# Flamingo block: the last quarter of the attention output added by VectorE from the PSUM bank, one operand sum moved ahead of a multiplication, and another finish of the last group

## The chip, the core and the metric

The kernel runs on one core of a Trainium2 chip. A core has a matrix engine (TensorE, PE in the profile, with its weight loads PEld), three elementwise engines (VectorE or DVE, ScalarE or ACT, GpSimd or POOL) and SyncE (SP), whose queue issues transfers. Each engine works through its own queue in order and waits on semaphores for the others. The metric is the time on the device, in microseconds; the median of three runs of the kernel before is 1302.78 us (1302.33 to 1303.58).

## What is computed

The reference, cut to what matters:

```python
def xattn(x, context, Wq, Wk, Wv, Wo, bo):           # 16 heads of 64
    q, k, v = heads(x @ Wq), heads(context @ Wk), heads(context @ Wv)
    attn = softmax(q @ k.T / 8)
    return merge(attn @ v) @ Wo + bo
def ffn(x, W, b, logits, u):
    idx = argmax(log_softmax(logits) - log(-log(u)))
    return x @ W[idx] + b[idx]
y   = x + tanh(g_xattn) * xattn(layernorm(x), ctx_768)
out = y + tanh(g_ffn)   * ffn(layernorm(y))
```

x has 4 x 2048 rows of 512 features, the context 4 x 77 rows of 384, all in float32.

## The kernel before

**Groups.** The 8192 rows of x are worked through in 16 groups of 512 rows. Rows tiles (`xg`, `ys`, `ts_`) hold rows on partitions, column tiles (`xc`, `pT`) hold features on partitions; VectorE's 32x32 block transposes lead from one to the other (`to_columns`, `to_rows`). The head projections are folded into matrices ahead of the groups: `m` (x to the scores of all heads) and `vo` (probabilities to the attention output), so that a group is three matmuls: scores (`ps_s`), attend (`ps_a`) and the feed-forward part (`ps_f`).

**Seven products.** Each of the three is done by a scheme with seven block products in place of eight (class `Seven`). The moving operand is cut into four blocks: B11, B12, B21, B22, the first digit half of the contraction, the second half of the group's 512 rows. GpSimd forms four sums of them (`Columns.sum`, line 437):

```python
a, b_, op = dict(T1=("B12", "B11", ALU.subtract), T2=("B22", "T1", ALU.subtract),
                 T3=("B22", "B12", ALU.subtract), T4=("B21", "T2", ALU.subtract))[name]
```

The products go in the order B11, T1, T2, B21, T3, B22, T4 (`ORDER`) into three PSUM banks. The four quarters of the result (11, 22, 12, 21: output half, then row half) become ready one after another. `post(s)` evicts after product s: after products 0, 1, 2 and 6 ScalarE copies a bank into the tile `snap` (`keep`; for attend with the bias `bo_c`, as two activations, line 473; otherwise line 469); after 3, 4 and 5 VectorE adds a bank to what is in `snap` (line 486). Quarter 21 is the last; it is the whole bank `ps[0]` after product 6.

**A group.** The main loop (i = 1 to 15, j = i-1, f = i-2) runs the scores of group i, the attend of group j, whose softmax was done before, and the feed-forward of group j. While the attend products run, ScalarE forms the exponentials of group i head by head (`exps`, line 532), VectorE sums each of four head sets (`head_sum`, lines 539 and 540), and GpSimd multiplies by the reciprocals (`head_scale`, line 543). VectorE then transposes the probabilities into columns for the next attend (`p_columns`, line 552). When quarters of the attend are ready, GpSimd adds them to the columns of x, which turns `xc[j]` into y (`residual`, line 558), then forms T1 to T4 of y for the feed-forward, while `y_rows` transposes y to rows for the second layernorm and the last addition. The seventh feed-forward product runs in the next group (`end_of_ff`).

The order of all this is written out by hand: the statements after `at.product(s)` and `ff.product(s)` fix the place of each instruction in its engine's queue. What follows the attend of a group is lines 868 to 881: on VectorE the sum of the last heads; on GpSimd residual 12, T1, T2, residual 21, the last heads' multiplication, T3, T4. Groups 3, 7 and 11 also reload `m` and form its block sums (`weight_sum`, line 124), one of them on VectorE at line 869.

**The end.** After the loop, lines 907 to 947 do the attend of the last group, lines 949 to 970 its feed-forward, with the layernorm statistics of y between the products: `mean` and `var` each put a small matmul (`ps_st`, line 375) into PE's queue; `rstd` ends in a power on GpSimd (line 409). Lines 972 to 981 then scale the feed-forward rows, add them to y and store: rows blocks 8 to 15 by ScalarE and GpSimd, 0 to 7 by VectorE in eight fused operations (line 976), in twelve DMAs on the queues of SyncE and ScalarE.

Of the kernel before, what the change touches and what calls it, by code (L numbers as in the profile page):

```python
# [10 lines left out]
AF = mybir.ActivationFunctionType  # L11
ALU = mybir.AluOpType
AX = mybir.AxisListType

P = 128
# [4 lines left out]
def flamingo_block_kernel(  # L20
# [43 lines left out]
    NA = 4  # L64
# [55 lines left out]
    def weight_sum(w, n, engine=None):  # L120

        to, a, b_, op = ((5, 0, 3, ALU.subtract), (3, 3, 2, ALU.add), (4, 3, 0, ALU.subtract),
                         (6, 1, 4, ALU.subtract))[n]
        (engine or nc.gpsimd).tensor_tensor(flat(w[:, to]), flat(w[:, a]), flat(w[:, b_]), op)  # L124
# [430 lines left out]
    def residual(j, at, which, engine=None):  # L555

        c = xc[j].at["B" + which]
        (engine or nc.gpsimd).tensor_tensor(c, c, at.quarter(which), ALU.add)  # L558

    def y_rows(j, q0, v=None):  # L560
        if j not in ys:
            ys[j] = row_tile("y")
        for q in (q0, q0 + 1):
            c = xc[j].all[:, q, :]
            to_rows(ys[j], c if v is None else c[:, ts(v, T2)], q, v)
# [190 lines left out]
    for i in range(1, NGRP):  # L756
        j, f, nx = i - 1, i - 2, i + 1
        n = norms[i]
        last = nx == NGRP
        swap_m, swap_vo = i % GPB == GPB - 1 and not last, 1 < i and j % GPB == 0  # L760
        if 1 < i:

            s0 = scores0(i)
            for s in range(6):
                s0.product(s)
                if s == 0:
                    s0.post(0)
                    if 0 <= f:
                        end_of_ff(f)
                    p_columns(j, 6, 8)  # L770
                    xc[i].sum("T4")
                if s == 1:
                    p_columns(j, 8, 10)
                    if 0 <= f:
                        f_rows(f, ff, 1)
                if s == 2:
                    pT[j].sum("T1")
                    pT[j].sum("T3")
                if 0 < s:
                    s0.post(s)  # L780
                if 0 <= f and s in (2, 3):
                    n.stats(ys[f], 0, 8 * (s - 2), 8)
                if s == 3 and 0 <= f:
                    add_bias(f, nc.gpsimd)
            for k in range(2):
                s_rows(i, k, s0.chunk(0, k))

            s1 = Seven("ps_s", w_scores, xc[i], (2, 3), SNAP)
            s2 = Seven("ps_s", w_scores, xc[i], (4,), SNAP1)
            for s in range(7):  # L790
                s1.product(s)
                s2.product(s)
                if s == 0:
                    s1.post(0)
                    s2.post(0)
                    s0.product(6)
                    s0.post(6)
                    n.mean()
                    for k in range(2):
                        s_rows(i, KH + k, s0.chunk(1, k))  # L800
                elif s < 4:
                    norm_step(n, s)
                if swap_vo and 3 <= s:
                    weight_sum(vo, s - 3, nc.vector if s < 5 else None)
                if 5 <= s and 0 <= f:
                    f_scale(f, n.rs, 5 * (s - 5), 5)
                if 0 < s:
                    s1.post(s)
                    s2.post(s)
                if s == 5:  # L810
                    for k in range(2):
                        s_rows(i, 2 + k, s1.chunk(0, k))
                    s_rows(i, 4, s2.chunk(0, 0))
            for k in range(2):
                s_rows(i, KH + 2 + k, s1.chunk(1, k))
            s_rows(i, KH + 4, s2.chunk(1, 0))
            if swap_m:
                load_m(nx // GPB)
        if not last:
            norms[nx] = Norms(nx)  # L820


        at = Seven("ps_a", w_attend, pT[j], (0, 1), SNAP, bo_c)
        for s in range(7):
            at.product(s)
            if s == 0:
                pT[j].sum("T2")
                if 0 <= f:
                    f_scale(f, n.rs, 10, 6)
                    f_add(f, 0, NG, nc.gpsimd)  # L830
                    store(f)
                head_max(i, 0)
                head_max(i, 1)
            if s == 1:
                head_max(i, 2)
                head_max(i, 3)
            if 1 <= s:
                e = (0, 10, 20, 32, 44, 56, 64)
                exps(i, e[s - 1], e[s])
            if s == 0 and i == 1:  # L840
                weight_sum(vo, 3)
                pT[j].sum("T3")
            if s == 1 and i == 1:
                scale_wf(wfr)
            if s == 2:
                pT[j].sum("T4")
                if swap_m:
                    weight_sum(m, 0)
                if not last:
                    x_columns(nx)  # L850
                    norms[nx].stats(xg[nx], norms[nx].x0, 0, 8)
                head_sum(i, 0)
                head_scale(i, 0)
            if s == 3:
                if not last:
                    norms[nx].stats(xg[nx], norms[nx].x0, 8, 8)
                    if nx + 1 < NGRP:
                        load(nx + 1)
            if s == 4:
                residual(j, at, "11")  # L860
                head_sum(i, 1)
                head_scale(i, 1)
            if s == 5:
                head_sum(i, 2)
                head_scale(i, 2)
                residual(j, at, "22")
            if s == 6:
                if swap_m:
                    weight_sum(m, 1, nc.vector)
                head_sum(i, 3)  # L870
                residual(j, at, "12")
            at.post(s)
        if j % GPB == GPB - 1:
            load_vo((j + 1) // GPB)
        yc[j] = Columns(xc[j].all, **{f"T{k + 1}": tq[:, k] for k in range(4)})
        yc[j].sum("T1")
        yc[j].sum("T2")
        residual(j, at, "21")
        head_scale(i, 3)
        yc[j].sum("T3")  # L880
        yc[j].sum("T4")


        ff = Seven("ps_f", w_ffn, yc[j], (0, 1), SNAP)
        for s in range(6):
            ff.product(s)
            if s < 2:
                y_rows(j, 2 * s)
            if not last:
                if s == 1:  # L890
                    xc[nx].sum("T1")
                if s == 2:
                    xc[nx].sum("T2")
                if s == 4:
                    if swap_m:
                        weight_sum(m, 2)
                    xc[nx].sum("T3")
                    if swap_m:
                        weight_sum(m, 3)
            if 2 <= s:  # L900
                k = (0, 2, 3, 5, 6)
                p_columns(i, k[s - 2], k[s - 1])
            ff.post(s)
        f_rows(j, ff, 0)
# [6 lines left out]
    for s in range(7):  # L911
# [24 lines left out]
            store(f)  # L936
        if s == 6:
            residual(j, at, "12")
            for q in (0, 2):
                y_rows(j, q, 1)  # L940
        if 0 < s:
            at.post(s)
    yc[j] = Columns(xc[j].all, **{f"T{k + 1}": tq[:, k] for k in range(4)})
    yc[j].sum("T1")
    yc[j].sum("T2")
    residual(j, at, "21")
    yc[j].sum("T3")
    yc[j].sum("T4")
    n = Norms(NGRP + 1)
    ff = Seven("ps_f", w_ffn, yc[j], (0, 1), SNAP)  # L950
    for s in range(7):
        ff.product(s)
        if s == 0:
            n.stats(ys[j], 0, 8, 8)
            y_rows(j, 0, 0)
        if s == 1:
            y_rows(j, 2, 0)
            n.stats(ys[j], 0, 0, 8)
            add_bias(j, nc.gpsimd)
        if s == 3:  # L960
            n.mean()
            n.spread()
        if s == 4:
            n.var()
            n.rstd()
        ff.post(s)
        if s == 4:
            f_rows(j, ff, 1, 1)
        if s == 5:
            f_rows(j, ff, 0, 1)  # L970
            f_rows(j, ff, 0, 0)
    f_scale(j, n.rs, 8, 8)
    f_rows(j, ff, 1, 0)
    f_add(j, 8, 8, nc.gpsimd)
    for g in range(8):
        nc.vector.scalar_tensor_tensor(ys[j][:, g, :], ts_[j][:, g, :], n.rs[:, g : g + 1], ys[j][:, g, :],
                                       ALU.mult, ALU.add)
        if g == 3:
            store(j, 0, 4, (nc.scalar, nc.sync))
    store(j, 8, 8, (nc.scalar, nc.sync))  # L980
    store(j, 4, 4, (nc.sync, nc.scalar))


# [39 lines left out]
```

## Time and profile before

| what | value |
| --- | --- |
| median of 3 runs | 1302.78 us |
| the profiled execution | 1302.34 us, span 1300.4 us |
| PE busy | 1260.2 us, 97% of the span |
| POOL, DVE, ACT busy | 894.2, 884.8, 651.6 us |
| granted TensorE clock, mean | 0.993 |
| one group, start of a product to the same one of the next | 73.57 us |
| POOL sums T1 to T4 of 128x512 (line 437) | 1.27 us each |
| POOL residual of 128x512 (line 558) | 1.33 us mean of 64 |
| POOL multiplication of one head set (line 543) | 2.27 us |
| last matmul ends, span ends | 1288.7, 1300.4 us |

Times in profile rows are microseconds from the start of the span. A row of the timeline gives the start, the time covered, the engine, the line, the operation, what it writes and reads, and how many instructions were merged into it; square brackets hold the idle time ahead of it and what ended it. Matmul ends are modelled, so a row of PE reaches a little over the start of the next. A float32 matmul of the program is two instructions; one feed-forward product is eight of them.

### The profile page before, as it was taken

To read this page: it belongs to the slowest core of one execution; us is meant where nothing else is said; L and a number is where in the kernel's file an instruction comes from. 1 tells how busy PE (TensorE), PEld (TensorE's weight loads), DVE (VectorE), ACT (ScalarE), POOL (GpSimd) and SP (SyncE) were. 2 spreads that over 40 slices of the span, in tenths; PEclk is the share of its full clock that TensorE was granted. 3 is DMA by queue.
4 is the path that set the end of the run, shared out by engine and by line. 5 is a ranking of instruction groups with operands and counts; after the bars stand their busy time and mean duration, and the time that the engine had idled before them with its cause. 6 is when DMAs were issued, how large, how long until landed. Compare 5 with 4: busy or idle time off the path is not lost.

```text
span 1300.4 us, 16961 instructions
## 1 busy us (share of the span) xinstructions
PE 1260.2 (97%) x5780; PEld 1068.9 (82%) x5780; DVE 884.8 (68%) x1823; ACT 651.6 (50%) x1766; POOL 894.2 (69%) x495
## 2 busy tenths in 40 slices
PE   9999869999999999999999999999999999999996
PEld 5666658888888888888888888888888888888885
DVE  6669776766667676766667676666767676666556
ACT  4436482644628273653728273563818264463822
POOL 5332478585977788585986788585985888585765
PEclk9999989999999999999999999999999999999998
DMA  9775310112305030022304120032304111010102
GB/s 237 254 254 160 116 33 1 37 29 81 65 1 121 26 65 1 18 48 81 66 1 106 41 55 12 3 64 74 73 1 99 48 35 31 1 33 1 33 1 65
DMA packets 95285, 80.28 MB, mean 62 GB/s; under 512 B 3920, under 2 KB 83152, under 8 KB 95200
## 3 DMA queue, kind: packets, MB, share of 16 engines
q1 hardware_dynamic: 92528, 76.61, 22.9%
q10 hardware_dynamic: 2064, 1.47, 0.4%
q0 software_dynamic: 608, 1.13, 0.4%
q8 instruction: 46, 0.75, 0.2%
q14 instruction: 39, 0.32, 0.1%
HBM read 44.07 MB, written 35.13 MB: 61 GB/s over the span
## 4 chain that ended last, share of the span: by engine, by line
PE 62%; ACT 14%; POOL 13%; DVE 6%; DMA 2%; issue 2%; SPq 0%; DVEq 0%; POOLq 0%; ACTq 0%
PE ps_s L463 36%; PE ps_a L463 16%; ACT s L532 12%; PE ps_f L463 7%; POOL xc L558 5%; POOL tq L437 4%; POOL s L543 4%; DVE sm L539 2%; PE ps_vo L336 1%; ACT snap L473 1%; PE ps_kv L270 1%; DMA xg<-in_x_dram 1%; DMA wq<-in_WqT_dram 1%; PE ps_m L301 1%; DVE s L515 1%
## 5 line engine op out<-in xcount | busy, mean ns | idle before, releaser
L463 PE MATMUL ps_a<-pT,vo 128*128 128x256 f32 x2240 | 491.2, 381 | 14.4 <-ACT snap L473 7.6
L463 PEld LDWEIGHTS ps_a<-pT,vo 128*128 128x128 f32 x2240 | 426.9, 191 | 75.3 <-POOL wf L124 7.9
L532 ACT ACTIVATE s<-s,nmx,up 128x77 f32<-128x77 f32 x1024 | 355.7, 446 | 6.0 <-DVE nmx L526 6.0
L463 PE MATMUL ps_s<-tq,m 128*128 128x256 f32 x1280 | 294.1, 380 | 0.2 <-DVE m L124 0.2
L437 POOL TENSOR_TENSOR pT<-pT 128x1280 f32<-128x1280 f32 x64 | 186.8, 2920 | 131.7 <-PE ps_a L463 111.3
L463 PEld LDWEIGHTS ps_s<-tq,m 128*128 128x128 f32 x1280 | 241.6, 190 | 35.0 <-issue 2.4
L469 ACT COPY snap<-ps_s 128x512 f32<-128x512 f32 (+1 forms) x188 | 94.4, 511 | 310.4 <-DVE t L417 124.2
L463 PE MATMUL ps_s<-xc,m 128*128 128x256 f32 x960 | 222.9, 381 | 0.6 <-DVE wq L339 0.6
L463 PEld LDWEIGHTS ps_s<-xc,m 128*128 128x128 f32 x960 | 180.8, 190 | 28.9 <-DVE wq L339 2.3
L543 POOL TENSOR_TENSOR s<-s,sm 128x1232 f32<-128x1232 f32 x64 | 145.2, 2268 | 73.9 <-DVE sm L540 64.6
L486 DVE TENSOR_TENSOR snap<-snap,ps_s 128x512 f32<-128x512 f32 (+1 forms) x141 | 83.6, 594 | 91.3 <-PE ps_s L463 91.3
L515 DVE STREAM_TRANSPOSE s<-snap 128x512 f32<-128x512 f32 x156 | 100.0, 686 | 49.3 <-ACT snap L469 47.4
L539 DVE TENSOR_REDUCE sm<-s 128x16 f32<-128x1232 f32 x64 | 91.7, 1432 | 56.8 <-ACT s L532 56.8
L463 PE MATMUL ps_f<-tq,wf 128*128 128x256 f32 x512 | 120.3, 383 | 8.0 <-POOL tq L437 8.0
L578 ACT ACTIVATE t<-t,rs 128x128 f32<-128x128 f32 x248 | 75.8, 390 | 98.7 <-POOL rs L409 98.7
L463 PEld LDWEIGHTS ps_f<-tq,wf 128*128 128x128 f32 x512 | 95.7, 190 | 27.5 <-POOL tq L437 15.2
L402 POOL TENSOR_TENSOR rs<-rs,neghalf 128x16 f32<-128x16 f32 x16 | 50.2, 3136 | 93.6 <-DVE rs L399 93.6
L552 DVE STREAM_TRANSPOSE pT<-s 128x512 f32<-128x512 f32 x160 | 101.0, 678 | 13.8 <-POOL s L543 13.8
L437 POOL TENSOR_TENSOR tq<-xc,tq 128x512 f32<-128x512 f32 x64 | 81.5, 1273 | 32.6 <-PE ps_f L463 25.6
L473 ACT ACTIVATE snap<-ps_a,bo_c 128x256 f32<-128x256 f32 x128 | 53.7, 470 | 90.0 <-PE ps_a L463 54.4
L437 POOL TENSOR_TENSOR tq<-xc 128x512 f32<-128x512 f32 x64 | 81.3, 1270 | 24.1 <-DVE xc L412 18.1
L524 DVE TENSOR_REDUCE ps_st<-s 128x16 f32<-128x1232 f32 x64 | 92.4, 1444 | 2.1
(121 smaller groups left out, 1200.9 us busy)
## 6 DMA issues: line engine op xcount, KB each, us to landing
xg<-in_x_dram SPq DMA_DIRECT2D x64, 256.0 KB, 5.6
out_dram<-y SPq DMA_DIRECT2D x60, 256.0 KB, 4.0
vo<-vo_d SPq DMA_DIRECT2D x16, 640.0 KB, 5.4
m<-m_d SPq DMA_DIRECT2D x12, 640.0 KB, 3.9
vo_d<-vo SPq DMA_DIRECT2D x10, 512.0 KB, 3.4
m_d<-vo SPq DMA_DIRECT2D x4, 960.0 KB, 8.0
vo_d<-wq SPq DMA_DIRECT2D x6, 512.0 KB, 2.8
wq<-in_WqT_dram SPq DMA_DIRECT2D x8, 256.0 KB, 8.1
```

Source lines behind the costliest of these rows:

```text
L437: (engine or nc.gpsimd).tensor_tensor(self.at[name], self.at[a], self.at[b_], op)
L463: nc.tensor.matmul(self.ps[r][:, n, :], self.w(blk, c, pair), self.cols(cname, c), start=(first and n == 0 and c == 0), stop=(c == h - 1), ...
L469: nc.scalar.copy(dst, self.ps[r])
L473: nc.scalar.activation(dst[:, n, :], self.ps[r][:, n, :], AF.Identity, scale=1.0, bias=self.bias[:, q : q + 1])
L486: nc.vector.tensor_tensor(c, c, self.ps[r], ALU.add)
L515: nc.vector.transpose(key_chunk(sc[i], k), cols.rearrange("p (g h r) -> p g h r", h=HA, r=R))
L524: nc.vector.tensor_reduce(mx, head(i, h), AX.X, ALU.max)
L532: nc.scalar.activation(head(i, h)[:, g, :], head(i, h)[:, g, :], AF.Exp, scale=norms[i].up[:, g : g + 1], bias=nmx[h][:, g : g + 1])
L539: nc.vector.tensor_reduce(sm, head(i, h), AX.X, ALU.add)
L543: nc.gpsimd.tensor_tensor(head(i, h), head(i, h), sums[h].unsqueeze(2).to_broadcast([P, NG, J]), ALU.mult)
L552: nc.vector.transpose(pT[i].all[:, k, :].rearrange("p (g h r) -> p g h r", h=HA, r=R), key_chunk(sc[i], k))
L578: nc.scalar.activation(ts_[f][:, g, :], ts_[f][:, g, :], AF.Copy, scale=rs[:, g : g + 1])
```

## The change

In every group, quarter 21 of the attend is no longer copied to `snap` by ScalarE and added by GpSimd. VectorE adds the PSUM bank and the bias to the columns of x directly, in two fused operations of 128x256 (`residual_last`), placed ahead of the last heads' sum. On GpSimd T3 comes ahead of the last heads' multiplication.

In the last group the same is done for quarter 21. The transposes of y and the statistics are all placed behind the first feed-forward product, the mean's small matmul comes behind the third product instead of the fourth and the variance's behind the fourth instead of the fifth, and the bias is added in two halves. The rows are finished by quarters (output half by row half): one by GpSimd, two scaled by ScalarE and added by VectorE, and the last, transposed straight from the PSUM bank, by VectorE in eight fused operations of 64 features. The rows are stored as two halves, in eight DMAs.

```diff
+    def residual_last(j, at):
+
+        c = xc[j].at["B21"]
+        for n, pair in enumerate(at.pairs):
+            q = pair + NDC // 2
+            nc.vector.scalar_tensor_tensor(c[:, n, :], at.ps[0][:, n, :], bo_c[:, q : q + 1], c[:, n, :],
+                                           ALU.add, ALU.add)
...
             if s == 6:
                 if swap_m:
                     weight_sum(m, 1, nc.vector)
+                residual(j, at, "12")
+                residual_last(j, at)
                 head_sum(i, 3)
-                residual(j, at, "12")
-            at.post(s)
+            else:
+                at.post(s)
...
         yc[j].sum("T1")
         yc[j].sum("T2")
-        residual(j, at, "21")
+        yc[j].sum("T3")
         head_scale(i, 3)
-        yc[j].sum("T3")
         yc[j].sum("T4")
...
         if s == 6:
             residual(j, at, "12")
+            residual_last(j, at)
             for q in (0, 2):
                 y_rows(j, q, 1)
-        if 0 < s:
+        elif 0 < s:
             at.post(s)
...
+    def scaled(h, v, engine):
+
+        d, y = by_feature(ts_[j], h, v), by_feature(ys[j], h, v)
+        r = n.rs[:, ts(v, NG // 2)]
+        if engine is nc.vector:
+            for g in range(NG // 2):
+                nc.vector.scalar_tensor_tensor(y[:, g, :], d[:, g, :], r[:, g : g + 1], y[:, g, :],
+                                               ALU.mult, ALU.add)
+            return
+        if engine is nc.scalar:
+            for g in range(NG // 2):
+                nc.scalar.activation(d[:, g, :], d[:, g, :], AF.Copy, scale=r[:, g : g + 1])
+            return
+        engine.tensor_tensor(d, d, r.unsqueeze(2).to_broadcast(list(d.shape)), ALU.mult)
+        engine.tensor_tensor(y, y, d, ALU.add)
+
+    for s in range(6):
         ff.product(s)
         if s == 0:
             n.stats(ys[j], 0, 8, 8)
             y_rows(j, 0, 0)
-        if s == 1:
             y_rows(j, 2, 0)
             n.stats(ys[j], 0, 0, 8)
-            add_bias(j, nc.gpsimd)
-        if s == 3:
+            for v in (1, 0):
+                y = ys[j][:, ts(v, NG // 2)]
+                nc.gpsimd.tensor_tensor(y, y, bf_r.unsqueeze(1).to_broadcast([P, NG // 2, P]), ALU.add)
+        if s == 2:
             n.mean()
             n.spread()
-        if s == 4:
+        if s == 3:
             n.var()
             n.rstd()
         ff.post(s)
+        if s == 3:
+            f_rows(j, ff, 0, 0)
+            scaled(0, 0, nc.gpsimd)
         if s == 4:
             f_rows(j, ff, 1, 1)
+            scaled(1, 1, nc.scalar)
         if s == 5:
             f_rows(j, ff, 0, 1)
-            f_rows(j, ff, 0, 0)
...
+            scaled(0, 1, nc.scalar)
+    ff.product(6)
+    for k in range(2):
+        to_rows(ts_[j], ff.ps[0][:, k, :], 2 + k, 0)
+    scaled(1, 0, nc.vector)
+    store(j, 0, 8, (nc.sync, nc.scalar))
+    for h in (1, 0):
+        y = by_feature(ys[j], h, 1)
+        nc.vector.tensor_tensor(y, y, by_feature(ts_[j], h, 1), ALU.add)
+    store(j, 8, 8, (nc.sync, nc.scalar))
```

The removed lines 972 to 981 are told above and printed with the kernel.

More of the change, by code (lines that the diff above doesn't have):

```diff
@@ L938, in flamingo_block_kernel, with by_feature @@
             residual(j, at, "12")
+            residual_last(j, at)
             for q in (0, 2):
                 y_rows(j, q, 1)
-        if 0 < s:
+        elif 0 < s:
             at.post(s)
     yc[j] = Columns(xc[j].all, **{f"T{k + 1}": tq[:, k] for k in range(4)})
[L944 to L948, printed above, removed]
+    for t in ("T1", "T2", "T3", "T4"):
+        yc[j].sum(t)
     n = Norms(NGRP + 1)
     ff = Seven("ps_f", w_ffn, yc[j], (0, 1), SNAP)
-    for s in range(7):
+    def by_feature(t, h, v):
+        return t[:, ts(v, NG // 2), ts(h, D // NA // 2)]
+    def scaled(h, v, engine):
[13 more added lines that the diff above has]
+    for s in range(6):
         ff.product(s)
@@ L966, in flamingo_block_kernel @@
         ff.post(s)
+        if s == 3:
+            f_rows(j, ff, 0, 0)
+            scaled(0, 0, nc.gpsimd)
         if s == 4:
             f_rows(j, ff, 1, 1)
+            scaled(1, 1, nc.scalar)
         if s == 5:
             f_rows(j, ff, 0, 1)
-            f_rows(j, ff, 0, 0)
[L972 to L981, printed above, removed]
+            scaled(0, 1, nc.scalar)
[8 more added lines that the diff above has]
+    store(j, 8, 8, (nc.sync, nc.scalar))
 def kernel(x, ctx_768, g_xattn, g_ffn, L0_xattn_Wq, L0_xattn_Wk, L0_xattn_Wv, L0_xattn_Wo, L0_xattn_bo,
```

## Prediction

> **What bounds the kernel now.** I read the page's busy shares first, then PE's waits, then one group's end on PE, GpSimd (POOL) and VectorE (DVE), then the last 60 us.
>
> ```profile
> PE 1260.2 (97%) x5780; PEld 1068.9 (82%) x5780; DVE 884.8 (68%) x1823; ACT 651.6 (50%) x1766; POOL 894.2 (69%) x495
> ...
> PEclk9999989999999999999999999999999999999998
> ```
>
> PE is busy 97% of the span at nearly full clock; no other engine passes 69%. Only PE's gaps, its start and what follows its last matmul can be shortened. PE's waits, in total over the run:
>
> ```profile
> PE ps_f L463 <- POOL tq L437: 8.0, 18, 0.7
> ```
>
> That is one wait in each group, 18 times because groups 3, 7 and 11 have two; the next longest (7.6 us, for ACT's snap) happens once, where the change touches nothing. Group 4's end on PE (start, duration, count):
>
> ```profile
> 419.63 1.89 PE L463 MATMUL ps_f<-xc,wf 128*128 128x256 f32 x8
> 421.36 3.62 PE L463 MATMUL ps_f<-tq,wf 128*128 128x256 f32 x16
> 424.81 1.89 PE L463 MATMUL ps_f<-xc,wf 128*128 128x256 f32 x8
> 427.04 1.99 PE L463 MATMUL ps_f<-tq,wf 128*128 128x256 f32 x8 [0.34 <-POOL tq L437]
> 428.87 1.89 PE L463 MATMUL ps_f<-xc,wf 128*128 128x256 f32 x8
> ```
>
> A product of the last matmul (8 instructions) takes 1.73 us from start to start (419.63 to 421.36). The fifth, which reads T3, was due at 424.81 + 1.73 = 426.54 and starts at 427.04: 0.50 late. It then takes 1.83 instead of 1.73 (to 428.87). One wait costs 0.60. POOL's queue:
>
> ```profile
> 417.11 2.50 POOL L558 TENSOR_TENSOR xc<-xc,snap 128x512 f32<-128x512 f32 x2
> 419.69 1.27 POOL L437 TENSOR_TENSOR tq<-xc 128x512 f32<-128x512 f32 x1
> 421.04 1.27 POOL L437 TENSOR_TENSOR tq<-xc,tq 128x512 f32<-128x512 f32 x1
> 422.27 1.26 POOL L558 TENSOR_TENSOR xc<-xc,snap 128x512 f32<-128x512 f32 x1
> 423.50 2.26 POOL L543 TENSOR_TENSOR s<-s,sm 128x1232 f32<-128x1232 f32 x1
> 425.72 1.27 POOL L437 TENSOR_TENSOR tq<-xc 128x512 f32<-128x512 f32 x1
> ```
>
> These are residuals 22 and 12, T1, T2, residual 21, the last head's multiplication, T3. T3 ends at 426.99, just before PE resumes. Its operands were there at 419.6; it is late only by its place.
>
> **The loop, part by part.** POOL loses residual 21 and takes T3 before the multiplication, so T3 ends at about 423.5 instead of 426.99, 3.0 us ahead of its due time. The multiplication keeps its start, 423.5, and T4 ends one 1.23 us slot earlier. ACT loses two evictions (0.84 us), and its first copy of the next matmul still starts behind PE's first product, so that is worth nothing.
>
> VectorE gains two 128x256 operations that read the PSUM bank. No row has this form. Below: the eviction-add from PSUM takes 0.69 for 512 elements and 0.233 for 64 (L388), about 1.02 ns an element, so 0.43 for 256 and, overlapping, 0.85 for the pair. Above, a rule that speaks against the change: the Trainium skill, Vector Engine (DVE) Microarchitecture Reference, section "Points that are easy to get wrong", says this kind of operation halves its rate with two non-bf16 SBUF sources. Two cycles an element would be 0.53 each and about 1.3 for the pair. But one source here is PSUM, and the nearest row with that mix (L392, 64 elements) takes 0.241 against 0.233 for the plain addition. I take 0.85.
>
> The pair waits for PE's seventh product, and behind it in VectorE's queue stand the last head's sum, the transposes of y and the transposes of P:
>
> ```profile
> 418.49 1.44 DVE L539 TENSOR_REDUCE sm<-s 128x16 f32<-128x1232 f32 x1 [2.29 <-ACT s L532]
> 419.96 0.25 DVE L540 RECIPROCAL sm<-sm 128x16 f32<-128x16 f32 x1
> 420.13 1.24 DVE L417 STREAM_TRANSPOSE y<-xc 128x512 f32<-128x512 f32 x2
> 423.57 1.30 DVE L417 STREAM_TRANSPOSE y<-xc 128x512 f32<-128x512 f32 x2 [2.20 <-POOL xc L558]
> 425.79 1.90 DVE L552 STREAM_TRANSPOSE pT<-s 128x512 f32<-128x512 f32 x3 [0.92 <-POOL s L543]
> ```
>
> ACT saw the bank ready at 419.88; VectorE waits to about 419.65-419.9. The pair ends near 420.6, the sum and reciprocal near 422.3 (now 420.2). POOL reaches the multiplication at 423.5 anyway: 1.2 us of cover. If it were gone, P's transposes move one for one; ACT's first copy of the next scores (behind their chain, 432.92 to 433.50) must precede PE's third scores product (435.8, now 0.6 sooner), another 1.7. The transposes of y fill 422.3 to 424.8 (now until 424.87), because B21 no longer comes late from POOL. So P's transposes start as now, at 425.8.
>
> What is late next on PE? T1: it ends at 420.96, PE takes it some 0.05 later, it is due at 421.36: slack 0.35. T2: 0.75. ACT's copy of the second T2 product (425.09 + 0.58) frees the bank for the T3 product with 0.87 to spare. All hang on PE's own attend products earlier in the group, so none loses slack as groups become shorter.
>
> Sum: groups 2, 4, 5, 6, 8, 9, 10, 12, 13, 14 and 15 (eleven) 0.60 each = 6.6. Group 1: due 204.53, started 205.09, 0.66. Groups 3, 7, 11: due 648.26, started 648.99 in group 7, 0.83 with the slow restart, 2.5 together. Their other wait, T1 behind m's block sum on VectorE, stays. Loop: **-9.75 us**; without the restart's 0.1 it is -8.25.
>
> **The end.** I use times of before, without the loop's shift. PE's seventh attend product ends at 1276.2. Now B12 and B22 are transposed at 1274.04, ahead of that; after the change these four stand behind the PSUM pair. Pair to 1277.1, transposes 1.42 to 1278.5, statistics 1.6 to 1280.1, four more transposes 1.45 to 1281.5, statistics 1.6 to 1283.1, their total 0.2 to 1283.3. PE's small matmul for the mean moves from behind the fourth ff product to behind the third, which ends at 1281.2. So PE, which does not wait there now, waits till 1283.35 and takes its fourth product at 1283.6. The rest (four products, the variance's matmul, restart 0.1) ends at 1291.0 instead of 1288.74: 2.3 later.
>
> A rule against this: the Trainium skill, TensorE: Matmul & The Clock Gate, "Part 1", puts the clock at half after an idle window of some 3.4 us. The trace had gaps of 2.69 and 2.84 us on PE (before 151.26 and 165.13) with the granted clock at 1.00, and 0.50 only after one of 7.57. A 2.2 us gap should leave it alone; at half clock 32 instructions of 0.216 would take 6.9 us more.
>
> Behind PE the chain is shorter. Today:
>
> ```profile
> 1288.81 0.58 ACT L469 COPY snap<-ps_f 128x512 f32<-128x512 f32 x1 [6.75 <-PE ps_f L463]
> ...
> 1290.31 4.28 DVE L976 SCALAR_TENSOR_TENSOR y<-t,rs,y 128x128 f32<-128x128 f32 x8
> ...
> 1291.87 2.57 POOL L582 TENSOR_TENSOR y<-y,t 128x1024 f32<-128x1024 f32 x1 [3.49 <-ACT t L578]
> ```
>
> Seven of the eight start 0.264 apart; the eighth lasts 2430 ns against a median of 347, as long as POOL's addition beside it. Rows are complete at 1294.6, 5.9 after PE. The last transfers run from 1295.2 to 1299.0, 0.79 MB at some 205 GB/s; the span ends at 1300.4.
>
> After: two transposes from the bank to 1291.9 (no copy), eight half-size operations at 0.20 to 0.26 apart (to 1293.6-1294.0), half the rows stored, two 128x512 additions of some 0.65 to 1295.0, the other half. POOL must be done before these eight: variance at 1285.45, power 2.91 to 1288.9, two operations of 1.27 to 1291.5; the bias in two halves (2.3 each) ends by 1285.5, before the power. It is just clear. ACT has two times eight activations of about 0.28 from 1289.1, to 1293.8, in time for the additions. Eight stores of 128 KB replace twelve; all 1.05 MB now leave from 1294.3: 5.1 us at that rate, to 1299.4 against 1299.0. The end: **+0.4**, from -0.7 (small operations at 0.15, faster queues) to +2 (0.35 each, or held by POOL).
>
> Net -9.75 + 0.4 = -9.35. The profiled run took 1302.34 (span 1300.4 and 1.9 around it): 1293.0. The median of the runs is 0.44 above it; the same difference from 1302.78 gives **1293.4**.
>
> **Rivals.** (1) Slower: the pair holds the SBUF port that POOL needs, at half rate. It would start at T1's moment and delay T1 by about 1.25; less slack 0.35 and plus the restart that is 1.0 a group, 12 us in twelve groups: -9.75 + 12 + 0.4 = +2.6, **1305.4**. It decides from a pair of some 1.1 us. For it: m's block sum on VectorE, two SBUF inputs, stretched POOL's two residuals from 2.50 to 3.75 in group 7. Against: additions with one source in PSUM lie inside POOL operations without stretching them (406.88 within a 2.27 multiplication). With the port held at full rate, T1 is 0.76 late, 0.5 a group, 6 us: 1299.5. (2) The clock falls in the last products: +6.9 at most, 1300.3. (3) T3 comes early and the product still starts late, for another source: loop 0, end +0.4: 1303.2. The rows above give every other source at least 0.35.
>
> **How the numbers follow.** Main case 0.85, 1292.0 to 1295.6 (loop -8.25 to -10, end -0.7 to +2); port at full rate 0.04; clock 0.04; (3) 0.04; port at half rate 0.03. The range goes to 1297 for a partly held port. A difference within 0.2% (2.6 us) can hardly be told from none: faster 0.89, same 0.08 (clock and (3)), slower 0.03.
>
> **What would show it.** Group period 72.97 instead of 73.57; PE's wait for POOL's tq left three times only (T1 in groups 3, 7, 11), unless T1 or T2 shows it; the pair at 0.43 each with T1 still 1.27; the multiplication still right behind T3; at the end a PE gap near 2.2 us before the mean's matmul, clock 1.00, and stores leaving within 3 us of the last matmul. I am wrong if T1 stretches, if P's transposes start later against PE, or if the end grows by over 2 us.

## The result and the profile after

| kernel | median, us | ratio to before, 95% interval | span of the profiled run | clock |
| --- | --- | --- | --- | --- |
| before | 1302.79 (4 runs) | | 1300.4 | 0.993 |
| after | 1293.83 (4 runs, 1292.68 to 1294.91) | 0.993 [0.9918, 0.9943] | 1291.6 | 0.993 |
| after, measured again beside the last experiments | 1296.46 (5 runs, 1293.50 to 1297.81) | 0.9947 [0.9933, 0.9961] | 1294.2 | 0.994 |

The change is faster: by 9.0 us in the first measurement, by 6.3 us in the second (before at 1302.71 there). The forecast was 1293.4. What the second measurement has on top is told, as far as a trace shows it, with the experiments on the end.

PE's waits after the change (engine and operation, whom it waited for; us in total, times, longest). The line on `ps_f` is the one shown for before, where it read 8.0 us in 18 waits:

```profile
PE ps_st L375 <- DVE tot L374: 3.8, 4, 2.0
...
PE ps_f L463 <- POOL tq L437: 2.2, 3, 0.7
```

The three that are left are T1's in groups 3, 7 and 11, and the wait for the mean's total at the end, 2.0 us, is new. Group 4 on PE, the same products as shown before:

```profile
419.48 3.62 PE L463 MATMUL ps_f<-tq,wf 128*128 128x256 f32 x16
422.93 1.89 PE L463 MATMUL ps_f<-xc,wf 128*128 128x256 f32 x8
424.66 1.89 PE L463 MATMUL ps_f<-tq,wf 128*128 128x256 f32 x8
```

The T3 product starts 1.73 us after the one ahead of it, with no wait and no slow restart. GpSimd and VectorE beside it:

```profile
417.81 1.27 POOL L437 TENSOR_TENSOR tq<-xc 128x512 f32<-128x512 f32 x1
419.16 1.28 POOL L437 TENSOR_TENSOR tq<-xc,tq 128x512 f32<-128x512 f32 x1
420.39 1.28 POOL L437 TENSOR_TENSOR tq<-xc 128x512 f32<-128x512 f32 x1
421.63 2.27 POOL L543 TENSOR_TENSOR s<-s,sm 128x1232 f32<-128x1232 f32 x1
```

```profile
417.95 0.88 DVE L565 SCALAR_TENSOR_TENSOR xc<-ps_a,bo_c,xc 128x256 f32<-128x256 f32 x2 [3.63 <-PE ps_a L463]
418.75 1.43 DVE L539 TENSOR_REDUCE sm<-s 128x16 f32<-128x1232 f32 x1
```

T3 (third row of GpSimd) ends at 421.67, 3.0 us ahead of its product. VectorE's pair lies inside T1's row, and that still has 1.27 us. The wait of 3.63 us in front of the pair is for PE's seventh product and costs nothing.

Measured from the first feed-forward product of one group to that of the next, an ordinary group takes 72.97 us instead of 73.57, and groups 3, 7 and 11 take 73.97 instead of 74.81. The first attend product and the last group's first feed-forward product mark the ends of the loop, before:

```profile
151.26 5.18 PE L463 MATMUL ps_a<-pT,vo 128*128 128x256 f32 x20 [2.69 <-issue]
...
1276.03 1.89 PE L463 MATMUL ps_f<-xc,wf 128*128 128x256 f32 x8
```

and after:

```profile
151.67 11.03 PE L463 MATMUL ps_a<-pT,vo 128*128 128x256 f32 x40 [2.69 <-issue]
...
1266.42 1.89 PE L463 MATMUL ps_f<-xc,wf 128*128 128x256 f32 x8
```

Between them lie 1124.77 us before and 1114.75 after, which is 10.02 less. The profiled run of after starts this stretch 0.41 us later, though all lines ahead of the loop are the same; at the last group it is therefore 9.61 us ahead. From there to the end of the span it takes 25.18 us, before 24.37. 0.41 - 10.02 + 0.81 = -8.80 is the whole difference of the spans.

### The profile page after: what moved, and what is told of

Its sections match the earlier page's. It is cut to its first block, busy times and chain, and to the rows that moved or that the text cites. A ratio compares the mean times of both kernels' runs of the same rounds, so it can differ in the third digit from the quotient of the medians.

```text
span 1291.6 us, 16923 instructions
## 1 busy us (share of the span) xinstructions
PE 1259.6 (98%) x5780; PEld 1072.1 (83%) x5780; DVE 892.2 (69%) x1857; ACT 639.3 (49%) x1741; POOL 875.2 (68%) x481
## 4 chain that ended last, share of the span: by engine, by line
PE 86%; DVE 4%; ACT 4%; DMA 2%; POOL 2%; issue 0%; SPq 0%; DVEq 0%; POOLq 0%; ACTq 0%
PE ps_s L463 36%; PE ps_a L463 32%; PE ps_f L463 14%; ACT s L532 4%; PE ps_vo L336 1%; PE ps_kv L270 1%; PE ps_m L301 1%; POOL xc L558 1%; DMA m<-in_Wk_dram 1%; DVE s L370 1%; DMA xg<-in_x_dram 1%; DVE s L515 1%; DVE sm L539 1%; DVE vo L124 1%; POOL s L543 1%
## 5 line engine op out<-in xcount | busy, mean ns | idle before, releaser
L463 PE MATMUL ps_f<-xc,wf 128*128 128x256 f32 x384 | 90.8, 379 | 0.0
```

The costliest lines, as they stand in the source:

```text
L463: nc.tensor.matmul(self.ps[r][:, n, :], self.w(blk, c, pair), self.cols(cname, c), start=(first and n == 0 and c == 0), stop=(c == h - 1), ...
```

## The experiments

Theory: PE waited for T3 in each group, and only that; each half of the loop's change alone may free T3, and the new end costs a little. Rivals: the new end gives part of the gain; VectorE's addition and T3's place are both needed; the addition on VectorE holds up GpSimd's operations beside it (called the port below); the clock falls in the new gap. Spans and periods below are those of profiled runs.

### Loop and end apart

**Loop of after, end of before:**

```diff
         if s == 6:
             residual(j, at, "12")
-            residual_last(j, at)
             for q in (0, 2):
                 y_rows(j, q, 1)
-        elif 0 < s:
+        if 0 < s:
             at.post(s)
...
-    scaled(1, 0, nc.vector)
-    store(j, 0, 8, (nc.sync, nc.scalar))
+    f_scale(j, n.rs, 8, 8)
+    f_rows(j, ff, 1, 0)
...
```

All lines behind the main loop are those of before.

> The loop of after with the end of before. My theory (all of the gain is PE's wait for T3 in 15 groups, the new end costs a little): group period 72.97 us, time 9.6 below before, about 1293.2. Rival (the new end gives part of the gain): clearly less than 9 us, above 1294.5.

Median 1292.76 us, ratio 0.9935 [0.9921, 0.9948]; period 72.97, groups 3, 7 and 11 73.97. All of the gain is in the loop.

**Loop of before, end of after** (the loop's lines are those of before, all lines behind it those of after):

> The loop of before with the end of after. My theory: period 73.57 as before, PE waits 2.0 us for the mean's total, the chain behind PE is 1.5 us shorter: 0.8 above before, about 1303.6. Rival (the new end gains): 1 us or more below before, 1301.8 or less.

Median 1304.83 us in 21 runs, 1.0016 [1.0009, 1.0022]. The sign is as expected and the size is not: 2.5 us instead of 0.8. The runs fall into two groups, seven from 1303.29 to 1303.71 and fourteen from 1304.42 to 1305.94. The profiled run is one of the second. Its PE rows from the mean's small matmul on, then its stretches of 1 us (length; busy time and instructions of PE, PEld, DVE, ACT, POOL; granted clock; DMA share, GB/s):

```profile
1283.42 0.39 PE L375 MATMUL ps_st<-tot,jm 128*128 128x16 f32 x2 [2.04 <-DVE tot L374]
1283.66 2.53 PE L463 MATMUL ps_f<-xc,wf 128*128 128x256 f32 x8
1285.99 0.44 PE L375 MATMUL ps_st<-tot,jm 128*128 128x16 f32 x2
1286.28 2.99 PE L463 MATMUL ps_f<-tq,wf 128*128 128x256 f32 x8
1289.10 1.89 PE L463 MATMUL ps_f<-xc,wf 128*128 128x256 f32 x8
```

```profile
1284.00:1285.00 1.00, 1.00 (x6) 0.90 (x5) 0.75 (x5) 0.00 (x0) 1.00 (x1) 0.97 0.00 0
1285.00:1286.00 1.00, 1.00 (x4) 0.72 (x4) 0.00 (x0) 0.00 (x0) 0.56 (x1) 0.50 0.00 0
1286.00:1287.00 1.00, 1.00 (x5) 0.91 (x4) 0.53 (x2) 0.00 (x0) 0.27 (x1) 0.50 0.00 0
1287.00:1288.00 1.00, 1.00 (x4) 0.82 (x3) 0.96 (x3) 0.00 (x0) 1.00 (x1) 0.50 0.00 0
1288.00:1289.00 1.00, 1.00 (x5) 0.83 (x5) 0.05 (x1) 0.00 (x0) 1.00 (x1) 0.82 0.00 0
```

Behind the gap of 2.04 us the granted clock is at 0.50 for some 3.4 us (by the shares in the rows, from 1284.94 to 1288.36). The fourth and fifth products, with the variance's small matmul, take 5.44 us (1283.66 to 1289.10). In after's first profile, with the clock at 1.00, they take 3.76 (1274.04 to 1277.80), 1.7 less:

```profile
1273.80 0.40 PE L375 MATMUL ps_st<-tot,jm 128*128 128x16 f32 x2 [2.03 <-DVE tot L374]
1274.04 1.97 PE L463 MATMUL ps_f<-xc,wf 128*128 128x256 f32 x8
...
1277.80 1.89 PE L463 MATMUL ps_f<-xc,wf 128*128 128x256 f32 x8
```

By these spans the new end costs 0.8 us with the clock at full and about 2.5 when it falls; the lower group of times lies 1.2 above before.

**The gap filled.** In both kernels with the new end, one extra product is put ahead of the mean's matmul (its bank is read by nobody; the rest is computed as it was):

```diff
         if s == 2:
+            for _ in range(1):
+                ps = bank("ps_x")[:, : 2 * T2].rearrange("p (n t) -> p n t", n=2)
+                for q in range(2):
+                    for c in range(2):
+                        nc.tensor.matmul(ps[:, q, :], w_ffn(4, c, q), yc[j]("T2", c),
+                                         start=(q == 0 and c == 0), stop=(c == 1), skip_group_check=True)
             n.mean()
             n.spread()
```

> The end-only kernel with the gap filled by an extra product, as in the filled kernel. If the two groups of times of the end-only kernel (about 1303.5 and about 1305) come from the clock that falls after PE's gap: all runs near 1303.5, at most one above 1304.4. If from elsewhere: half or more of them at 1304.4 to 1306.

> As after, but one extra feed-forward product (8 PE instructions, 1.73 us, its bank is read by nobody) stands in PE's gap ahead of the mean's matmul. If the gap's idle time makes the clock fall in some executions: none falls here, time 1293.0 and all runs within 1 us, while PE's last matmul ends where it does in after's profiled run. If the scatter of 2 us between executions of after and of the end-only kernel has another source, it stays here.

In the end-only kernel twelve of thirteen runs are now between 1302.98 and 1303.92, one at 1305.69; the median is 1303.43 (1.0005 [0.9997, 1.0014]), 1.4 us lower (1.8 against before of the same measurement), although PE has 8 more instructions. PE waits 0.30 us instead of 2.04, and the clock is 1.00 throughout its end:

```profile
1281.50 1.89 PE L993 MATMUL ps_x<-tq,wf 128*128 128x256 f32 x8
1283.70 0.40 PE L375 MATMUL ps_st<-tot,jm 128*128 128x16 f32 x2 [0.30 <-DVE tot L374]
1283.94 1.97 PE L463 MATMUL ps_f<-xc,wf 128*128 128x256 f32 x8
```

So the upper group came from the gap. The filled kernel with the new loop has a median of 1293.16 (0.9933 [0.9919, 0.9947]), four runs from 1293.02 to 1293.78 and one at 1295.62; single high runs also occur without any such gap (the loop-only kernel has one at 1297.04). No trace of such a run was kept. Its mean granted clock is 0.989 in the loop-only kernel, where the other four show 0.992 to 0.995, so a lower clock somewhere is a candidate; where is open. The first group is not what differs between the profiled runs: from the first attend product to the next group's first feed-forward product, all nine with VectorE's addition from the bank in the loop take 119.14 to 119.18 us. Ahead of it they do differ: that attend product starts between 151.0 and 152.6 us, for a reason that was not tried.

**After, once more:**

> The changed kernel itself, beside the others on one chip: 1293.8; with the gap's clock account, two groups near 1292.9 and 1294.7.

Median 1296.46, above the expectation. Its profiled run has a span of 1294.2, 2.6 us over the first profile's. 0.96 of them lie ahead of the groups (the first attend product starts at 152.63 instead of 151.67); behind the gap at the end, where the clock was at 0.50, lie the others. PE there:

```profile
1274.76 0.51 PE L375 MATMUL ps_st<-tot,jm 128*128 128x16 f32 x2 [2.04 <-DVE tot L374]
1275.11 3.55 PE L463 MATMUL ps_f<-xc,wf 128*128 128x256 f32 x8
```

The product takes 3.39 us to the next row (1278.50) instead of 1.81; from the last group's first feed-forward product to the end it is 26.82 us against 25.18, 1.64 more. The loop between takes 1114.75 us in both. Two of the five runs are higher still, 1297.35 and 1297.81, with mean clocks of 0.989 and 0.990; these two shares do not explain them.

**When the clock falls.** The clock fell in other places too. In after's first profile, PE's gaps of 2.69 us (the row at 151.67 above) and 2.84 us in the first group are each followed by stretches at half clock:

```profile
153.00:154.00 1.00, 1.00 (x4) 0.61 (x4) 1.00 (x3) 0.00 (x0) 0.00 (x0) 0.57 0.00 0
154.00:155.00 1.00, 1.00 (x4) 0.82 (x3) 1.00 (x1) 0.00 (x0) 0.92 (x1) 0.50 0.00 0
155.00:156.00 1.00, 1.00 (x4) 0.82 (x3) 0.97 (x2) 0.00 (x0) 1.00 (x1) 0.50 0.00 0
```

```profile
165.54 10.59 PE L463 MATMUL ps_a<-pT,vo 128*128 128x256 f32 x40 [2.84 <-POOL pT L437]
```

```profile
167.00:168.00 1.00, 1.00 (x4) 0.74 (x4) 1.00 (x3) 0.00 (x0) 1.00 (x1) 0.50 0.00 0
```

In the profile of before the same gaps left it at 1.00. Rows like these show when the clock changes. In each of the fourteen profiled runs, every fall and return of it up to PE's last matmul lies a whole number of steps of 3.413 us behind the first fall. In after they are at 153.14, 156.54, 166.78, 170.20, 180.44 and 187.26, which is 0, 1, 4, 5, 8 and 10 steps; in the end-only kernel the falls at 151.72 and 1284.94 are 332 steps apart. In the step ahead of each of the 35 falls PE was idle for 0.55 of it or more. Of all other steps at full clock, only three go beyond 0.53 (0.56, 0.56 and 0.58, all in after's second profile).

So it matters how a gap lies against these steps. In the end-only profile, 1.89 us of the gap at the end fall into one step (0.55), and the clock falls. In after's first profile the gap is divided between two steps (0.28 and 0.32), and the clock stays. As an estimate from these figures, a gap of 2.04 us at a random place puts 0.55 of a step into one step in about half of the executions; by the times it was 14 of 21. The idle shares rest on modelled matmul ends, and no run here moved a gap on purpose.

### The halves of the loop's change

**T3 ahead only**, quarter 21 as before:

```diff
         yc[j].sum("T2")
+        yc[j].sum("T3")
         residual(j, at, "21")
         head_scale(i, 3)
-        yc[j].sum("T3")
         yc[j].sum("T4")
```

> Only T3's place is changed: T1, T2, T3, residual 21, the multiplication, T4 on GpSimd; quarter 21 still goes through ScalarE and GpSimd. My theory (T3's place is the whole cause; the multiplication, 1.26 us later, is covered): period 72.97, 9.6 below before, 1293.2. Rival (VectorE's addition is needed, because otherwise P's transposes start 1.3 us later and something behind them stalls): PE shows a new wait, period between 73.0 and 74.2, gain under 6 us.

Median 1295.13, 0.9946 [0.9932, 0.9960]: 7.2 us, between the two expectations, and neither cause was right. Period 73.09 and 74.33. Residual 21 and the product that needs it:

```profile
422.09 1.27 POOL L558 TENSOR_TENSOR xc<-xc,snap 128x512 f32<-128x512 f32 x1
```

```profile
423.41 1.99 PE L463 MATMUL ps_f<-xc,wf 128*128 128x256 f32 x8
425.24 1.89 PE L463 MATMUL ps_f<-tq,wf 128*128 128x256 f32 x8
```

B21 is now complete only at 423.36, and its product, due at 423.41, starts at the right time but takes 1.83 instead of 1.73 us; in group 7 it starts late and loses 0.36. 12 x 0.12 + 3 x 0.36 = 2.5 us is what this kernel lacks. The multiplication and P's transposes, 1.2 us later, cost nothing, as the cover in the prediction says.

**VectorE's addition only**, T3 back behind the multiplication:

```diff
         yc[j].sum("T2")
-        yc[j].sum("T3")
         head_scale(i, 3)
+        yc[j].sum("T3")
         yc[j].sum("T4")
```

> VectorE's addition of quarter 21 stays, but T3 goes back behind the last heads' multiplication; end of before. My theory: the freed slot of 1.23 us alone puts T3's end 0.6 us ahead of its due time, so the wait goes here too: period 72.97, 9.6 below before, 1293.2; in groups 3, 7 and 11 with 0.3 us to spare at most. Rival (T3 must be moved ahead of the multiplication): the multiplication waits for the last heads' sum, T3 stays late, and at least half of the 0.5 us wait remains: gain under 5 us.

Median 1292.64, 0.9929 [0.9916, 0.9943]; periods 72.97 and 73.97, as in the loop-only kernel. T3 ends at 423.79 in group 4, its product starts at 424.34. The slot that residual 21 gave up is enough; T3's new place adds nothing to it.

### The port

ScalarE's two copies stay, and VectorE adds the copied quarter, so that both of its inputs lie in SBUF and none in a PSUM bank:

```diff
-                residual_last(j, at)
+                at.post(s)
+                residual(j, at, "21", nc.vector)
```

> As after, but the pair that reads the bank is replaced by ScalarE's two copies to snap and one VectorE addition of 128x512 with both inputs in SBUF. My theory of the port (only two SBUF inputs collide with GpSimd): the addition waits for T1's end and T2, which follows at once, then shows about 1.8 instead of 1.27 us; T1 and PE's due times are only just kept, the time within 1 us of after's 1293.8. Rival (the port costs nothing here either): T2 stays at 1.27. If PE gets a wait for T2 of over 0.2 us in twelve groups, the form with PSUM was worth 3 us or more.

GpSimd's T2 in group 4, beside an addition with two SBUF inputs on VectorE:

```profile
419.36 1.60 POOL L437 TENSOR_TENSOR tq<-xc,tq 128x512 f32<-128x512 f32 x1
```

```profile
419.08 0.74 DVE L558 TENSOR_TENSOR xc<-xc,snap 128x512 f32<-128x512 f32 x1 [4.55 <-ACT snap L473]
```

(The 4.55 us ahead of it, for ScalarE's copies, cost nothing.) T2 takes 1.60 instead of 1.28: the collision exists, though smaller than expected; the addition starts 0.2 us before T1's end, and T1 keeps its 1.27. Ordinary groups keep 72.97; groups 3, 7 and 11 grow from 73.97 to 74.34, 1.1 us in all. In group 7 the addition starts first, at 637.99, and there it is T1, for which PE waits, that is stretched:

```profile
638.17 1.64 POOL L437 TENSOR_TENSOR tq<-xc 128x512 f32<-128x512 f32 x1
```

Median 1295.49, 0.9951 [0.9937, 0.9965], with a scatter of 4 us. The form with PSUM, which leaves T1 at 1.27 in both kinds of group, is worth about 1 us by the periods; the times can't tell it.

### Two further edits

**The mean later** at the end (with GpSimd's quarter behind the power):

```diff
-        if s == 2:
+        if s == 3:
             n.mean()
             n.spread()
-        if s == 3:
+        if s == 4:
             n.var()
             n.rstd()
         ff.post(s)
+        if s == 4:
+            scaled(0, 0, nc.gpsimd)
         if s == 3:
             f_rows(j, ff, 0, 0)
-            scaled(0, 0, nc.gpsimd)
```

> As after, but at the end the mean's small matmul comes behind the fourth feed-forward product (and the variance's behind the fifth), as in the kernel before, with GpSimd's quarter behind it. My theory: PE's gap falls from 2.0 to about 0.4 us, its last matmul ends 1.7 us sooner, VectorE's last eight then wait for GpSimd's quarter, which holds the port until the same moment as now; 0.5 us faster than after with the clock at full, and no run with a fallen clock: median 1292.7, spread under 1 us. Rival (the gap doesn't matter): same as after.

Median 1293.76 (1293.06 to 1293.87), 0.993 [0.9916, 0.9944]. The gap is 0.31 us and the scatter 0.8, as expected; the 0.5 us gain over after's first measurement is missing. PE ends 0.9 us sooner instead of 1.7, because the variance's total now stands behind an eviction and two transposes on VectorE (a second wait of 0.52 us), so GpSimd's quarter starts 0.8 later and holds VectorE's last eight until its end:

```profile
1281.47 2.65 DVE L969 SCALAR_TENSOR_TENSOR y<-t,rs,y 128x64 f32<-128x64 f32 x8
1284.05 1.28 DVE L1013 TENSOR_TENSOR y<-y,t 128x512 f32<-128x512 f32 x2
```

The eight took 1.65 us in after.

**The block sum of m later**, added to that kernel:

```diff
-                if swap_m:
-                    weight_sum(m, 1, nc.vector)
                 residual(j, at, "12")
...
             if s < 2:
                 y_rows(j, 2 * s)
+            if s == 1 and swap_m:
+                weight_sum(m, 1, nc.vector)
```

> The end with the later mean, and in the loop m's block sum on VectorE in groups 3, 7 and 11 moved behind the transposes of y (behind the second feed-forward product), so that GpSimd's two residuals there are not held. My theory: T1's wait in these three groups (1.0 us each with its restart) goes: 3 us below the later-mean kernel, 1289.8. Rival (the block sum then holds the last heads' multiplication or T4, and P's transposes bring PE a new wait): no gain, or a wait at another product.

Median 1291.17, 0.9909 [0.9895, 0.9923]. Groups 3, 7 and 11 take 73.08 us instead of 73.97, 2.7 in all. In group 7 on GpSimd:

```profile
633.45 2.50 POOL L558 TENSOR_TENSOR xc<-xc,snap 128x512 f32<-128x512 f32 x2
...
642.06 2.52 POOL L437 TENSOR_TENSOR tq<-xc,tq 128x512 f32<-128x512 f32 x1
```

The two residuals are back from 3.75 to 2.50, and the block sum now holds T4, which takes 2.52 instead of 1.27 and has the time.

**The variance's total ahead of the eviction**, in the same kernel:

```diff
             n.spread()
+            tot = small.tile([P, n.n], F32, tag="tot1", name="tot")
+            nc.vector.tensor_reduce(tot, n.q, AX.X, ALU.add)
         if s == 4:
-            n.var()
+            nc.tensor.matmul(n.ps[:, 1], jm.rearrange("p a c -> p (a c)"), tot, start=True, stop=True)
             n.rstd()
```

> As the kernel with both edits, but at the end VectorE sums the variance's pairs before it evicts the fourth product, so that PE's second small matmul finds them ready. If that queue place is what kept the later-mean end from gaining: the power starts 0.6 to 0.8 us sooner, the port is free sooner, 0.6 below that kernel, 1290.5. If GpSimd's quarter or the stores set the end: no change, 1291.2.

Median 1290.47, 0.9907 [0.9892, 0.9922]: 0.7 lower in the medians, which the intervals can't tell apart; the second wait on PE is gone from the profile.

**The block sum later with the end of before:**

> The loop of after with m's block sum behind the transposes of y, and the end of the kernel before. If the end of before is the better one by 0.4 to 1.1 us, as the loop-only and the later-mean kernels say: 1290.1, the fastest of all. If the ends are equal: 1291.2, as the kernel with both edits.

Median 1290.21 (1290.05 to 1290.85), 0.9903 [0.9888, 0.9919], and PE's only wait for `ps_f` is one of 0.4 us in the first group. It is some 12.5 us below before and 3.6 below the first measurement of after, without any of the change's new end.

## Why the prediction was right, step by step

- **The wait for T3.** -9.75 us forecast, -10.02 measured over the loop. Ordinary groups -0.60 as forecast, which includes the slow restart of 0.1; groups 3, 7 and 11 -0.84 for -0.83; group 1, from its first attend product, -0.84 for -0.66 (119.99 us to 119.15). That the profiled run is 9.61 ahead at the last group, nearer still to the forecast, is luck: 0.41 us went ahead of the groups.
- **The pair on VectorE.** 0.85 forecast, 0.88 measured, 0.40 from start to start, below the 0.53 of the halved rate. T1's slack of 0.35 held in all ordinary groups.
- **VectorE's queue.** The sum and reciprocal end 2.1 us later against PE's products than before, inside the cover; in group 4 the multiplication follows T3 at once, at 421.63.
- **The slacks named** were incomplete: for T1, T2 and the bank I gave them, for B21 I did not. The T3-only kernel found it. It didn't matter to this change, because there B21 comes from VectorE.
- **PE's gap at the end.** Forecast 2.2 us, measured 2.03; PE's last matmul 2.3 us later, measured 2.30.
- **Behind PE.** The rows are complete 3.8 us after PE's last product (forecast 4.0), before 5.9. The DMA forecast held: the 1.05 MB move in some 5 us. The end in all: +0.4 forecast, +0.8 measured.
- **The clock: this step failed.** "A 2.2 us gap should leave it alone", with 0.04 for the opposite. The clock fell behind 2.04 us in after's second profile and in the end-only profile; by the times, in some two thirds of the end-only kernel's runs. The step rested on two longer gaps of the first group in one profile, and that they had kept the clock was luck: there each was divided between two steps of 3.41 us (idle shares 0.46 and 0.33, then 0.44 and 0.39). Behind the first of them the clock fell in eleven of the fourteen profiled runs. The price was 1.6 us rather than 6.9, because the clock came back after one step. That fits in the range. But the end of that second profile grew by 2.45 us (24.37 to 26.82), more than the 2 us that the prediction itself named as a sign of being wrong. Together with the 0.96 us ahead of the groups it explains a run at 1296.5; the highest runs it does not explain.
- **The range.** Its parts (loop -8.25 to -10, end -0.7 to +2) add up to 1292.1 to 1296.5, where the prediction gives its main case 1292.0 to 1295.6.
- **The port** behaved as in the main case for the pair, and as in the rival for an addition with two SBUF inputs.

The number was near for the right reason in the loop; at the end one cost, the clock's, was ruled out on too little evidence, and whether a run pays it is chance.

## What to carry to other kernels

When one engine is busy 97% of the time, list each of its operands with due time and ready time: a wait of about half a microsecond in each of 15 groups, with the slow restart behind it, was worth 10 us, and the next due operand (B21, 0.05 us away in one variant) decides which of several equal-looking edits keeps the gain. An edit that frees a queue slot and one that changes the order can be substitutes; try each alone before keeping both. A new idle gap of 2 us on the matrix engine can cost another 1.7 us through the clock, in some executions and not in others, so one profile at full clock does not clear it. An operation with two SBUF inputs on VectorE should not stand beside the GpSimd operation that is due next.

## What the hardware showed that was not expected

- The granted clock fell to 0.50 for about 3.4 us behind a PE gap of 2.04 us, in some executions and not in others of the same kernel. In these profiles it changes only at steps of 3.413 us, and in the step ahead of a fall PE was idle for 0.55 of it or more. The Trainium skill, TensorE: Matmul & The Clock Gate, "Part 1", speaks of an idle window of about 3.4 us that runs freely: the length and the free run agree with the traces, but here a step that was idle for little more than half of its length was enough.
- The halved rate that the prediction weighed was not seen even with two float32 SBUF sources: the eight operations of 64 features start about 0.20 us apart, those of 128 features before 0.264. The 64 more elements cost 1.05 ns each, as many as in an operation with PSUM (1.02), where half the rate would be about 2.
- An addition with two SBUF inputs didn't slow GpSimd evenly: it stretched the GpSimd operation that started after it (T2 1.60 for 1.28 in group 4, T1 1.64 for 1.27 in group 7) and not the one that already ran (T1 in group 4). In the other direction, with the later mean, GpSimd's addition, started just before, held VectorE's last eight (2.65 for 1.65).
